# Moving the 20-token tile from the last block of each layer to the first

## The chip, the cores and the metric

The kernel runs on one core of a Trainium2 chip. Its time is the device time of one execution in microseconds (us). Five engines work side by side, each through its own list of instructions in order: TensorE (PE: matmuls and transposes; PEld is its loading of stationary operands), VectorE (DVE), ScalarE (ACT), GpSimd (POOL) and SyncE (SP). POOL issues the indirect DMAs, SP and ACT plain ones. Engines meet only through semaphores.

## The reference

Two layers of a graph transformer over 2708 tokens of 512 numbers, with 8 heads of 64, everything in float32. One layer is, in essence:

```python
mask = adj + eye(n)
q, k, v = h @ Wq.T + bq, h @ Wk.T + bk, h @ Wv.T + bv      # 8 heads
scores = q . k / 8, set to -1e9 where mask == 0
ctx = softmax(scores) @ v
h1 = layer_norm(h + ctx @ Wo.T + bo)
ff = relu(h1 @ W1.T + b1) @ W2.T + b2                      # 512 -> 2048 -> 512
h2 = layer_norm(h1 + ff)
```

The adjacency is sparse: a token has a handful of neighbours, so scores are needed for a few keys of each token only. The same adjacency serves both layers, and the output of the first is the input of the second.

## The kernel before, in words

**Tokens by rank.** The program turns each row of the adjacency into a list of neighbours, and sorts the tokens by the length of their list, longest first. The 2708 tokens make NT = 22 tiles of 128, of which the last, tile 21, holds only 20 tokens; these have the shortest lists of all. `CAPS` holds the number of list slots of each tile: 22 for tile 0, then 14, 13, 12, down to 5 for tile 20 and 3 for tile 21. `ident_i` and `idx` say which token has which rank, and which rows its neighbours are. `FIRST` is the number of tiles, from the end, whose part of these tables is made ready first (`ranked`, `listed`), so that attention can begin with them.

**Attention of a tile** goes by chunks of two slots (`SLOTS`): a POOL indirect DMA fetches for each slot one row of keys and values for each of the tile's tokens (`loads`, L1004); VectorE multiplies by q and sums over each head (L1041, L1047); one step later ACT takes the exponent and scales half of the values (L1060, L1067), and VectorE scales the other half and adds up (L1073, L1080); two and three steps later the sums are closed (L1088 to L1103) and ACT divides (L1111), which gives cx. `attend` runs this as a sequence of steps. It is advanced by credit (`advance`, `PACE`) between the pieces of other work and holds at most two finished tiles ahead; `through(k)` runs it on until block k is done. Three chunks are fetched ahead (`EARLY`), into five or more buffers.

**Blocks.** The 22 tiles are worked in 11 blocks of two, in the order of the list `blocks`, which is the subject of the change; `order` is the same list tile by tile, and attention runs through it. For a block, `attended` transposes cx (L1166), projects by Wo and normalizes to h (L1293, then `norm`: L1150 to L1160); `turned` transposes h to hT; `feed_forward` makes 16 groups pf of 128 hidden units (L1351, over the block's 256 columns at once), which ACT evicts through relu as ft (L1359), and accumulates each tile's 512 outputs in `a` (L1324), three groups late. While block k is in its feed-forward, at group 10 or 11 the next block's cx is taken, projected and normalized, so that its hT is there when block k ends. In layer 0 the keys and values of the next layer are projected for block k in the groups 5 to 8 of block k + 1 (`keys_values`, L1407, L1410), and scattered to DRAM. In layer 1 the queries of later tiles are projected inside the blocks (`queries`, L1264).

**The small tile.** A tile of at most 32 tokens fills only a quarter of TensorE's columns. For it, four matmuls of a contraction go side by side into four column groups of the array, each with its own 32 rows of the output (`project` at L571, and `quarters` at L1339); VectorE then adds the four parts, three adds more than for a full tile (`plus_rest`: L586, or L588 where a scale goes with it).

**Who sets the order.** The instruction lists of TensorE, ACT and SP follow the program text (`by_hand`). VectorE's and POOL's lists are written in the order that a scheduler chooses; VectorE's and POOL's parts at the start and between the layers lie in a `manual_schedule`, but VectorE's list still shows chunks of one tile ahead of sums of another. Once built, each list is run in order.

**The two ends.** Before the first block of layer 0, TensorE projects keys, values and queries of all tokens (L576 in `first` and `first_queries`), while VectorE and ACT make the lists. Queries of the first four tiles are made from their own rows (`own_query`, L976) and not fetched from DRAM. Between the layers, the two queries of the first tiles are projected, then the last block's keys and values, then ten more queries, two of them early, while attention of layer 1 starts; its first gathers wait for the last keys in DRAM. The output rows go out by an indirect DMA (L1379). Behind it stands a slower version of the whole program (`by_rows`), which runs only where a list is too long for its slots; here it is skipped.

Of the kernel before, what the change touches and what calls it, by code (L numbers as in the profile page):

```python
# [45 lines left out]
QT = 6  # L46
OWN = 13
EARLY = 3
FIRST = 5
PACE = (0.62, 0.72)  # L50


# [420 lines left out]
def by_edges(ctx: ExitStack, tc: tile.TileContext, x, xT, adj, layers, out, good):  # L473
# [11 lines left out]
    NT = (N + P - 1) // P  # L485
# [118 lines left out]
    def lists_of(pa):  # L604
# [151 lines left out]
        def ranked(hot, before, half):  # L756
# [49 lines left out]

            first, last = NT - FIRST, NT - 1
            rest = nc.gpsimd.dma_start(out=new[:LW, last, :], in_=rec_d[last * P :, :])
# [12 lines left out]
        def listed(start):  # L821

            ts = slice(NT - FIRST, NT) if start else slice(0, NT - FIRST)
            if not start:
# [604 lines left out]
    now = Layer(0, layers[0])  # L1429


    blocks = [(20, 19), (18, 17), (7, 9), (6, 10), (5, 11), (0, 16)]
    blocks += [(1, 15), (2, 14), (3, 13), (4, 12), (NT - 1, 8)]
    NB = len(blocks)
    order = [g for block in blocks for g in block]

# [102 lines left out]
    for n in range(NL):  # L1539
# [30 lines left out]
        for k, block in enumerate(blocks):  # L1570
# [4 lines left out]
            for f, zs in enumerate(now.feed_forward(block, hs, hT)):  # L1575
# [22 lines left out]
                if not last:  # L1598
# [9 lines left out]
                    if f == 1 and k in (1, 3):  # L1608
                        i, name, scale = (1, "bk", 1.0) if k == 1 else (0, "bq", DK**-0.5)
# [41 lines left out]
def gnn_transformer(tc: tile.TileContext, x, xT, adj, layers, out):  # L1651

    nc = tc.nc
    with tc.tile_pool(name="result", bufs=1) as result:
        good = result.tile([1, 1], F32, name="good")
        by_edges(tc, x, xT, adj, layers, out, good)  # L1660
        redo = result.tile([1, 1], I32, name="redo")
        nc.vector.tensor_scalar(redo, good, P - 0.5, None, ALU.is_lt)
        again = nc.values_load(redo[0:1, 0:1], min_val=0, max_val=1)  # L1663
        with tc.If(again > 0):
            by_rows(tc, x, xT, adj, layers, out)
# [41 lines left out]
```

## Time and profile before

| what | us |
|---|---|
| three runs: median (lowest to highest) | 1942.04 (1936.44 to 1943.61) |
| profiled execution, its own time | 1946.15 |
| span of the profile, first to last instruction | 1944.3 |
| TensorE busy / VectorE / ACT / POOL | 1858.4 / 1321.0 / 934.7 / 809.3 |
| first pf of layer 0, first pf of layer 1 | 286.8, 1232.9 |
| last matmul ends | 1925.8 |

A line of the timeline has the start, the length in us, the engine, the source line, the operation with output and inputs, the number of instructions merged into it and, in brackets, how long the engine had been idle before and what released it. A float32 matmul shows as two instructions. A line of the list of waits has the instruction that waited, what it waited for, the total, the number of times and the longest. Times are counted from the span's start.

### The profile page before, as it was taken

What the parts mean: (1) busy time and instruction counts of PE and PEld (TensorE: products, weight loads), DVE (VectorE), ACT (ScalarE), POOL (GpSimd) and SP (SyncE); (2) the same over time, 40 slices, a digit from 0 to 9 for tenths busy, and PEclk for the clock granted to TensorE, in tenths of its full rate; (3) what the DMA queues carried; (4) which work ended last, traced back from release to release, by engine and by line L of the source; (5) the groups of instructions that cost most, each with busy time, mean ns of one, the idle gap of its engine ahead of it and who ended that gap; (6) DMA issues with size and microseconds to landing.
All of it is one profiled execution on the core that took longest, in us unless ns stands there. A gap on an engine that the chain in (4) does not pass through costs nothing. (4 is left out here: it accounts for less than half of the span.)

```text
span 1944.3 us, 20898 instructions
## 1 busy us (share of the span) xinstructions
PE 1858.4 (96%) x6162; PEld 1096.7 (56%) x6162; DVE 1321.0 (68%) x2172; ACT 934.7 (48%) x3219; POOL 809.3 (42%) x710
## 2 busy tenths in 40 slices
PE   9998968999999999999999997999999999999996
PEld 4443435556656556665665553566666666666663
DVE  5885467768759687695841237696987998877421
ACT  4660236445546655574451113555475767654510
POOL 3113526535536555364410124344555775546101
PEclk9999979999999999999999998999999999999998
DMA  9998848555646656554401478656665766643000
GB/s 322 355 314 299 275 136 302 172 179 184 205 138 201 217 188 197 177 183 154 146 17 65 136 246 325 202 197 204 203 222 168 251 222 220 209 155 125 17 6 14
DMA packets 131486, 366.92 MB, mean 189 GB/s; under 512 B 16668, under 2 KB 37004, under 8 KB 128654
## 3 DMA queue, kind: packets, MB, share of 16 engines
q0 software_dynamic: 69120, 246.35, 38.0%
q1 hardware_dynamic: 53332, 99.66, 14.8%
q10 hardware_dynamic: 8910, 19.48, 2.6%
q8 instruction: 50, 0.82, 0.2%
q14 instruction: 74, 0.61, 0.1%
HBM read 314.62 MB, written 50.83 MB: 188 GB/s over the span
## 5 line engine op out<-in xcount | busy, mean ns | idle before, releaser
L1004 POOL DMA_INDIRECT kv<-kv_d,idx x420 | 547.0, 1302 | 452.2 <-DVE acc L1080 273.5
L1351 PE MATMUL pf<-hT,w 128*128 128x256 f32 (+1 forms) x2816 | 637.2, 373 | 7.2 <-ACT ft L1359 5.2
L1324 PE MATMUL a<-w,ft 128*128 128x512 f32 x1344 | 632.2, 596 | 5.3 <-ACT ft L1359 4.4
L1351 PEld LDWEIGHTS pf<-hT,w 128*128 128x128 f32 x2816 | 521.2, 191 | 186.6 <-issue 106.5
L1359 ACT ACTIVATE ft<-pf,b 128x256 f32<-128x256 f32 (+1 forms) x352 | 160.3, 460 | 458.5 <-PE pf L1351 458.3
L1041 DVE TENSOR_TENSOR kv<-kv,q 128x1024 f32<-128x1024 f32 (+3 forms) x222 | 254.2, 1157 | 169.2 <-DMA kv<-kv_d,idx 131.1
L1324 PEld LDWEIGHTS a<-w,ft 128*128 128x128 f32 x1344 | 253.2, 191 | 198.6 <-issue 171.6
L1067 ACT ACTIVATE kv<-kv,p 128x64 f32<-128x64 f32 x1232 | 311.0, 335 | 5.0
L1047 DVE TENSOR_REDUCE sc<-kv 128x16 f32<-128x1024 f32 (+3 forms) x222 | 253.8, 1153 | 1.5
L1080 DVE TENSOR_TENSOR acc<-acc,kv 128x1024 f32<-128x1024 f32 (+2 forms) x178 | 204.0, 1146 | 18.9 <-ACT kv L1067 17.0
L1156 POOL TENSOR_TENSOR rd<-va,mhalf 128x1 f32<-128x1 f32 (+1 forms) x88 | 90.4, 1028 | 274.6 <-DVE va L1154 273.7
L576 PE MATMUL o<-wo,cT 128*128 128x512 f32 x336 | 151.1, 602 | 0.5 <-ACT cT L1171 0.5
L1073 DVE TENSOR_TENSOR kv<-kv,p 128x512 f32<-128x512 f32 (+1 forms) x178 | 121.4, 682 | 34.6 <-ACT p L1060 34.6
L1060 ACT ACTIVATE p<-sc,minus 128x8 f32<-128x8 f32 x420 | 102.8, 294 | 69.2 <-DVE sc L1047 62.1
L1111 ACT ACTIVATE cx<-acc,su 128x64 f32<-128x64 f32 (+1 forms) x352 | 88.5, 334 | 74.7 <-DVE su L1103 57.6
L576 PEld LDWEIGHTS o<-wo,cT 128*128 128x128 f32 x336 | 64.5, 193 | 83.2 <-issue 72.9
L681 ACT ACTIVATE code<-aj 128x2708 bf16<-128x2708 int32 (+1 forms) x22 | 73.3, 3332 | 49.2 <-POOL aj L677 49.0
L684 DVE MAX8 tops<-code 128x8 f32<-128x247 f32 (+2 forms) x242 | 83.1, 401 | 19.3 <-ACT code L681 19.3
L1160 DVE SCALAR_TENSOR_TENSOR h<-h,rd,ln_b 128x512 f32<-128x512 f32 (+1 forms) x88 | 65.6, 747 | 40.6 <-POOL rd L1156 40.6
L1067 ACT ACTIVATE acc<-kv,p 128x64 f32<-128x64 f32 (+1 forms) x352 | 88.8, 334 | 1.4
L1410 ACT COPY kvs<-v 128x512 f32<-128x512 f32 (+1 forms) x22 | 12.9, 586 | 158.9 <-PE v L576 138.5
L1375 DVE TENSOR_TENSOR h<-a,h 128x512 f32<-128x512 f32 (+1 forms) x44 | 29.9, 679 | 85.2 <-PE a L1339 48.8
(154 smaller groups left out, 1560.2 us busy)
## 6 DMA issues: line engine op xcount, KB each, us to landing
aj<-in_adj SPq DMA_DIRECT2D x21, 1354.0 KB, 8.4
kv_d<-kvs ACTq DMA_DIRECT2D x21, 512.0 KB, 7.4
w<-in_W SPq DMA_DIRECT2D x20, 512.0 KB, 6.5
xg<-in_xT SPq DMA_DIRECT2D x19, 512.0 KB, 8.6
kv<-kv_d,idx POOLq DMA_INDIRECT x420, 5.8
w<-in_W ACTq DMA_DIRECT2D x12, 512.0 KB, 7.2
q_d<-qs SPq DMA_DIRECT2D x22, 256.0 KB, 3.4
zT_d<-zT SPq DMA_DIRECT2D x22, 256.0 KB, 4.3
```

The lines of the kernel that those rows point to most:

```text
L576: nc.tensor.matmul(o[:r], xs(c), wm[:, c, :], start=(c == 0), stop=(c == NC - 1))
L1004: nc.gpsimd.indirect_dma_start(out=to, out_offset=None, in_=table[:, :], in_offset=bass.IndirectOffsetOnAxis(ap=s, axis=0), bounds_check=N ...
L1041: nc.vector.tensor_tensor(kv[:r, :c, :DM], kv[:r, :c, :DM], self.q[:r].unsqueeze(1).to_broadcast([r, c, DM]), ALU.mult,)
L1047: nc.vector.tensor_reduce(self.sc[:r, s0 : s0 + c, :], kv[:r, :c, :DM].rearrange("p s (h d) -> p s h d", d=DK), AX.X, ALU.add,)
L1060: nc.scalar.activation(p[:r, s, :], self.sc[:r, s, :], AF.Exp, bias=minus[:r, g, s : s + 1])
L1067: nc.scalar.activation(to[:, i, hd], kv[:r, i, DM + h * DK : DM + (h + 1) * DK], AF.Copy, scale=p[:r, s0 + i, h : h + 1],)
L1073: nc.vector.tensor_tensor(to[:, 0, :].rearrange("p (h d) -> p h d", d=DK), kv[:r, 0, DM:].rearrange("p (h d) -> p h d", d=DK), p[:r, s0, : ...
L1080: nc.vector.tensor_tensor(self.acc[:r, :c, :], self.acc[:r, :c, :], kv[:r, :c, DM:], ALU.add)
L1156: nc.gpsimd.tensor_tensor(rd[:r], va[:r], mhalf[:r], ALU.pow)
L1324: nc.tensor.matmul(a[:r], fts[f][:, c0 : c0 + r], self.w2[f // 2][:, f % 2, :], start=(f == 0), stop=(f == NFC - 1),)
L1351: nc.tensor.matmul(pf[:, :w], self.w1[f // 2][:, c, f % 2 * P : f % 2 * P + P], hT[:, c, :w], start=(c == 0), stop=(c == NC - 1),)
L1359: nc.scalar.activation(ft[:, :w], pf[:, :w], AF.Relu, bias=self.b1[:, f : f + 1])
```

## The change

The list of blocks is written in another order. Tile 21 (20 tokens) with tile 20 becomes the first block of each layer; tiles 19 and 18 the second; then (8, 9), (7, 10), (6, 11), (0, 17), (1, 16), (2, 15), (3, 14), (4, 13), (5, 12). Before, tile 21 stood with tile 8 in the last block. In chunks the blocks were 6, 8, 10, 11, 11, 15, 11, 11, 10, 11, 7, and are now 5, 7, 10, 10, 11, 15, 11, 11, 10, 10, 11. `FIRST` goes from 5 to 4, since the first four tiles of the order are now the last four by rank. How the small tile is computed stays as it was.

```diff
-FIRST = 5
+FIRST = 4
...
-    blocks = [(20, 19), (18, 17), (7, 9), (6, 10), (5, 11), (0, 16)]
-    blocks += [(1, 15), (2, 14), (3, 13), (4, 12), (NT - 1, 8)]
+    blocks = [(NT - 1, NT - 2), (NT - 3, NT - 4)] + [
+        (i, NT - 5 - i) for i in (*range(8, 5, -1), *range(6))
+    ]
     NB = len(blocks)
     order = [g for block in blocks for g in block]
```

## The prediction

> **What bounds the kernel now.** I read the page's busy shares, then the list of what TensorE waited for, then TensorE's timeline through the two places where those waits lie, then VectorE's timeline there. The chain that ended last reaches back only to 1932 us (the output's scatter), so the bound is argued from TensorE. Page and waits of TensorE:
>
> ```profile
> PE 1858.4 (96%) x6162; PEld 1096.7 (56%) x6162; DVE 1321.0 (68%) x2172; ACT 934.7 (48%) x3219; POOL 809.3 (42%) x710
> ...
> PE tp L1166 <- ACT cx L1111: 25.5, 4, 14.2
> PE tp L1166 <- DVE h L1160: 10.1, 4, 3.7
> ...
> PE pf L1351 <- ACT ft L1359: 5.2, 3, 2.9
> ```
>
> TensorE works 1858 of 1944 us; some 19 us of the rest is the tail after its last matmul (1925.8 us). Elsewhere it waits mainly for attention (cx) and for the norm behind it (h), at the start of each layer. TensorE's timeline there, layer 0, then layer 1 from 1200 us:
>
> ```profile
> 263.15 1.91 PE L1166 MATMUL tp<-ident,cx 128*128 128x128 f32 x4 [14.21 <-ACT cx L1111]
> ...
> 286.81 9.03 PE L1351 MATMUL pf<-hT,w 128*128 128x256 f32 x32 [0.46 <-ACT hT L1171]
> ...
> 332.60 1.04 PE L1166 MATMUL tp<-ident,cx 128*128 128x128 f32 x8
> ...
> 357.86 0.66 PE L1166 MATMUL tp<-ident,h 128*128 128x128 f32 x4 [3.14 <-DVE h L1160]
> ...
> 365.20 7.07 PE L1351 MATMUL pf<-hT,w 128*128 128x256 f32 x32
> ...
> 1211.87 1.91 PE L1166 MATMUL tp<-ident,cx 128*128 128x128 f32 x4 [7.43 <-ACT cx L1111]
> ...
> 1232.91 7.17 PE L1351 MATMUL pf<-hT,w 128*128 128x256 f32 x32 [1.05 <-ACT hT L1171]
> ...
> 1303.59 6.64 PE L1351 MATMUL pf<-hT,w 128*128 128x256 f32 x30
> ```
>
> The rows at 286.81, 365.20, 1232.91 and 1303.59 are the starts of the first and second feed-forward block of each layer. Between 248.3 and 410 us TensorE is idle for 30 us in all, and for 14 us between 1174 and 1233. From then on it runs without a gap over 4 us. So: whatever starts the *second* block of a layer sooner, measured against the TensorE work still left, shortens the kernel. VectorE in the stretch that makes cx late:
>
> ```profile
> 253.19 1.23 DVE L1041 TENSOR_TENSOR kv<-kv,q 128x1024 f32<-128x1024 f32 x1 [4.63 <-DMA kv<-kv_d,idx]
> 260.22 0.69 DVE L1041 TENSOR_TENSOR kv<-kv,q 128x512 f32<-128x512 f32 x1 [1.21 <-DMA kv<-kv_d,idx]
> 1193.19 1.22 DVE L1041 TENSOR_TENSOR kv<-kv,q 128x1024 f32<-128x1024 f32 x1 [5.15 <-DMA q<-q_d]
> ```
>
> By buffer names these three belong to tile 18, of the second block: the scheduler put them ahead of tile 19's sums, so the first block waits for a transfer that it doesn't need.
>
> **What the skill says here.** "TensorEngine Tiling (Array Packing)", section PSUM Bottleneck: packing small matmuls speeds up TensorE and leaves the emptying of PSUM as it was. The trace agrees, and more: 64 packed matmuls of the 20-token tile (L1339) take 8.4 us, 131 ns each, against 632.2/1344 = 470 ns for a full tile (L1324); but an add of 20x512 on VectorE takes 0.68 us, as one of 128x512 does, and each packed result needs three more of them (L586, L588). So the small tile is cheap on TensorE and dear on VectorE; the forecast goes by that. "TensorE: Matmul & The Clock Gate", section on HAM oscillation, says that idle gaps above about 3.4 us drop the clock: after the 14.21 us gap four transposes took 1.91 us, not 0.60, and the granted clock was 0.65 in 250 to 260 us. I price a long gap at its length plus 1 to 2 us.
>
> **The change, part by part.**
>
> *TensorE's work* is the same in total but for 2.7 us (tile 21's own query in layer 0: 1.05 us for 3.44, and smaller transposes). It moves: with 148 columns a feed-forward block costs 37.0/2 = 18.5 us for pf and 15.0 + 4.2 us for a, 37.7 in all, against 30.0 + 30.1 = 60.1. So the first block loses 22.4 us and the last gains them; with the output projection (1.05 for 3.6 us) and transposes, **25.1 us** of work move from ahead of the second block to behind it, 27.5 in layer 1 with tile 21's query.
>
> *Attention ahead of the blocks.* A chunk is two slots. Before, the first two blocks need 6 and 14 chunks; now 5 and 12. FIRST 4 instead of 5 follows the tiles that start first; one copy smaller, nothing I price.
>
> *Layer 0, first block.* The instruction order of the changed kernel has no chunk of tile 19 ahead of tile 20's sums. Walking VectorE's list with the durations above: tile 21's first product at 221 (q needs three more adds, 2.1 us), tile 20's last chunk at 240, its sums at 246, cx on ACT by 249: where TensorE now arrives (248.3 less 2.7) and waits 2 to 3 us instead of 14.2. The projections end at 257, then VectorE has two products of tile 19 in front (4.9 us), tile 21's h with three adds (6.5) and tile 20's (4.3): 270, and the first block starts at about **272**, 15 us sooner than 286.8.
>
> *Layer 0, second block.* Here the cover is thin. TensorE would reach the transposes of cx after 12 steps of 2.1 to 2.4 us, near 300. VectorE must first do, from 270: three adds for a query, tile 19's last chunk, tile 18's four, their sums, and three chunks of tile 8 that the list puts ahead: 33.6 us by summing its list, plus about 5 us of gather waits (6 us were lost so in 300 to 320), so cx of tile 18 comes at about 308 to 310 against 325.1 (cx of tile 17). ACT holds its ft evictions in order behind that, so TensorE stands still at about the sixth to eighth step: about 15 us lost. From cx to the next block took 40 us before (325.1 to 365.2), paced by the norm's chain; I take 36, as the remaining steps are shorter: second block at **346**. Sum: 346 - 365.2 + 25.1 = **+6** us (bounds 0 to +12, as 340 or 352).
>
> *Keys and values of the first block* (L1407) then need six more adds on VectorE (4.3 us) before their PSUM is free, while TensorE gets there 4.9 us sooner (k, v of tile 21 take 2.1 us, not 7.0). Before, it waited 2.05 us there. I add **+2** (0 to +10; the list holds two chunks fewer ahead of them).
>
> *Between the layers* the last block is now full. Its norm is hidden by two queries, one of which shrinks from 3.44 to 1.05 us, so 1 to 2 us show, while tile 21's seven adds are gone from there: **+0.6**. All keys are still written by the same amount of TensorE work.
>
> *Layer 1.* The query of tile 19 is fetched on SP two q stores sooner than tile 18's was, so the 5.15 us wait should go; cx of tile 20 comes at about 1200 (layer's own time kept), TensorE's queries end at 1201, projections end at 1207, h at 1214 behind two queries: first block at **1216.6** against 1232.9. Tile 18's cx at 1249 (30 us of VectorE after the first ft, as before), TensorE there at 1246, 3 us lost; second block at **1273.5** against 1303.6. Sum: -30.1 + 27.5 = **-2.6** (bounds -8 to +4). The window for the third block's ten chunks shrinks from 82 to 70 us; VectorE needs about 64 with norms and queries (10 x 4.5 + 19): **+1.5** (0 to +6).
>
> *Tail.* VectorE's chain after the last matmul loses three adds: **-2**.
>
> Sum: 6 + 2 + 0.6 - 2.6 + 1.5 - 2 = **+5.5 us** on the profiled execution's 1946.15 us (span 1944.3 and 1.85 around it), 1951.7; that execution lies 4.1 above the median 1942.04, so **1948** as a median. Likeliest case's own range: 1940 to 1955.
>
> **Rivals.**
>
> *The early start is kept (faster).* If attention's second block keeps up with the short first one, nothing is lost: second blocks at 319 and 1265 give -21 and -11. For it: ACT and gathers have room (48%, 189 GB/s). Against: VectorE is 87% busy in 1250 to 1600, and its 33.6 us list alone ends past 300. Half of that gain, with cx of tile 18 by 300, is about -14: 1928. It decides once the second block of layer 0 starts before 338.
>
> *VectorE becomes the bound at the start (slower).* The 15 added adds of tile 21 in layer 0, 10 us, fall where VectorE is busiest instead of at the end where it idles. If gathers stall as much as in 380 to 402 us (7 us of waits), the keys' wait costs +10, the second block slips to 352 (+6 more): +19 and so 1961.
>
> *Waits at the 15-chunk block* (tile 0; 3.75 and 2.66 us near 658 and 689) stay where they are, since the block keeps its place and its 15 chunks: zero.
>
> *The change doesn't take hold:* excluded, since in TensorE's list the first pf groups now have 148 columns.
>
> **How the numbers follow.** Likeliest case 0.50, early start kept 0.17, VectorE bound 0.33. A measurement of this kernel tells about 0.5%, 9.7 us, from no change (the three runs span 7). Faster by more than that: 0.12 of the 0.17. Slower: 0.31 of the 0.33 and 0.08 of the 0.50, so 0.39. Within: 0.49. Range for 8 in 10: 1929 to 1963, from the faster rival's centre to just past the slower one's.
>
> **What would show it.** First pf near 272 and 1217, with the 14.21 and 7.43 us waits gone; new waits of pf or a for ft (L1359) in the first block of layer 0, some 15 us; second pf rows near 346 and 1273; v (L576) waiting for kvs more than 2 us; a tail of 17 us. Wrong if the list's gathers land late, if the next 10-chunk windows of layer 1 show waits, or if VectorE is simply quicker than its list.

## The result, and the profile after

The changed kernel takes 1952.62 us (median of 16 runs, 1947.54 to 1957.56), the kernel before 1942.29 us (16 runs beside it). The ratio is 1.0053, 95% interval [1.0041, 1.0065]: slower by 10.3 us, just past the 0.5% named as the limit of what can be told. The profiled execution has an own time of 1954.57 us and a span of 1952.8, against 1946.15 and 1944.3: a difference in span of 8.5, which the bookkeeping below explains.

From the page of the changed kernel and from the list of what TensorE waited for (engine, operation and line; what it waited for; us in total, times, longest):

```profile
PE 1863.1 (95%) x6162; PEld 1097.8 (56%) x6162; DVE 1321.8 (68%) x2175; ACT 933.9 (48%) x3219; POOL 805.2 (41%) x710
...
PE tp L1166 <- DVE h L1160: 23.8, 9, 6.1
PE a L1339 <- ACT ft L1359: 22.8, 8, 5.4
...
PE pf L1351 <- ACT hT L1171: 4.4, 4, 2.8
...
PE tp L1166 <- ACT cx L1111: 3.8, 1, 3.8
...
PE v L576 <- DVE kvs L586: 1.5, 1, 1.5
```

The waits for cx are down from 25.5 us to 3.8. In their place stand 22.8 us of waits for ft at L1339, the packed second matmuls of the 20-token tile, and waits for h more than twice as long as before. TensorE's timeline (start, duration, operation, wait ahead of it) shows where: layer 0's first block, the start of its second, then layer 1's.

```profile
268.53 6.75 PE L1351 MATMUL pf<-hT,w 128*128 128x148 f32 x32 [0.46 <-ACT hT L1171]
...
282.53 1.89 PE L1339 MATMUL a<-w,ft 128*20 128x512 f32 x2 [5.42 <-ACT ft L1359]
...
303.93 2.17 PE L1339 MATMUL a<-w,ft 128*20 128x512 f32 x4 [5.23 <-ACT ft L1359]
...
337.03 1.12 PE L1166 MATMUL tp<-ident,h 128*128 128x128 f32 x4 [6.12 <-DVE h L1160]
...
347.16 7.07 PE L1351 MATMUL pf<-hT,w 128*128 128x256 f32 x32
...
1227.90 4.32 PE L1351 MATMUL pf<-hT,w 128*128 128x148 f32 x32 [0.55 <-ACT hT L1171]
...
1272.62 1.03 PE L1339 MATMUL a<-w,ft 128*20 128x512 f32 x2 [4.12 <-ACT ft L1359]
...
1294.34 7.07 PE L1351 MATMUL pf<-hT,w 128*128 128x256 f32 x32
```

Between layer 0's two pf rows TensorE is idle for 22.1 of 78.6 us, and its granted clock there (the share of full speed that the profile shows) is 0.79, against 0.93 in the first block before. The packed matmuls of a (L1339) also take longer: the same 64 add up to 20.6 us instead of 8.4, since the waits break them up (a piece of two takes 1.03 us at 1235.07, an unbroken eight 1.05 at 1291.54) and, in layer 0, the clock is lower. An ft waits because ScalarE works in program order, and attention stands ahead of it. ScalarE's timeline just ahead of the 5.42 us wait:

```profile
279.66 0.49 ACT L1060 ACTIVATE p<-sc,minus 128x8 f32<-128x8 f32 x2 [4.77 <-DVE sc L1047]
280.19 2.02 ACT L1067 ACTIVATE acc<-kv,p 128x64 f32<-128x64 f32 x8
282.11 0.36 ACT L1359 ACTIVATE ft<-pf,b 128x148 f32<-128x148 f32 x1
```

ScalarE waits 4.77 us for scores from VectorE, weighs a chunk, and only then evicts ft at 282.11; 0.4 us later TensorE goes on. So the wait named "ft" is a wait for attention. VectorE works without a gap from 267 to 288.7 us. Later in the block it is not full: of the 78.6 us it is busy for 59.5, and it waits 3.7, 3.9 and 6.4 us for gathered keys and values. The longest of these waits:

```profile
323.19 1.23 DVE L1041 TENSOR_TENSOR kv<-kv,q 128x1024 f32<-128x1024 f32 x1 [6.43 <-DMA kv<-kv_d,idx]
```

No run separates VectorE's own work from the gathers that feed it; "attention" below stands for both.

Where the 8.5 us come from. The third column is plain difference; the fourth is the TensorE work that the change has moved behind that point; the sum is what the kernel has really lost or gained by then. 25.1 and 27.5 are the prediction's; k and v of the first block add 4.9 (7.0 less 2.1 us) once passed, and o with its transposes for a full last block gives 2.7 back.

| Point, us | Before | After | Difference | Work moved | Net |
|---|---|---|---|---|---|
| layer 0, second pf | 365.20 | 347.16 | -18.0 | 25.1 | +7.1 |
| layer 0, third pf | 449.55 | 423.87 | -25.7 | 30.0 | +4.3 |
| layer 0, sixth pf | 696.24 | 676.91 | -19.3 | 30.0 | +10.7 |
| layer 0, last pf | 1088.62 | 1074.05 | -14.6 | 27.3 | +12.7 |
| layer 1, first pf | 1232.91 | 1227.90 | -5.0 | 5.0 | 0.0 |
| layer 1, second pf | 1303.59 | 1294.34 | -9.3 | 27.5 | +18.2 |
| last matmul of a, end | 1925.65 | 1939.40 | +13.8 | 0 | +13.8 |
| span | 1944.3 | 1952.8 | +8.5 | 0 | +8.5 |

The prediction's 22.4 us for a block's feed-forward was 1.8 too much: layer 1's last block takes 55.3 us from pf to end with 256 columns and 34.7 with 148, a difference of 20.6. (It added up durations of rows that overlap: in the third block a pf row of 1.89 us and an a row of 1.88 start 1.7 us apart.) With 1.8 taken off, the second pf of layer 1 stands at +16.4, and layer 0's rows would be lower by as much.

A single row is not exact. Two of the runs below have, for a while, the same instruction lists as one of the two kernels, so their profiles are second profiles of it. "The small tile in the second-last block" is the kernel before up to 845 us: its second, third and sixth pf come at 358.66, 446.22 and 693.04. "The change in layer 0 alone" is the changed kernel up to 1140 us: 346.58, 423.60, 673.39, and the last pf at 1071.68. With all four pairs of profiles, the net lies between 6.5 and 13.6 us at the second pf, and between 7.2 and 13.9 at the sixth. A difference of a few us at one row can be chance.

Layer 0 loses its 12.7 us mainly in three places: the first block (7.1, of which 2.8 come back in the second), the third (4.9) and the sixth (4.6, of which 2.2 come back in the seventh). The boundary gives it back: between the last pf of layer 0 and the first of layer 1 TensorE is idle for 14.4 us before and 7.4 after, its granted clock from the end of layer 0's last block is 0.92 before and 0.98 after, and 1.8 us of it are the prediction's overcount. Most of that gain belongs to layer 1's own short block: with layer 0 alone changed, 3.6 us come back there. Layer 1's first block loses it again. The rest of layer 1 loses nothing more, and the tail gives 5.3 us.

### The profile page after: what moved, and what is told of

It reads as the page before. It is cut to its first block, busy times and chain, and to the rows that moved or that the text cites. A ratio compares the mean times of both kernels' runs of the same rounds, so it can differ in the third digit from the quotient of the medians.

```text
span 1952.8 us, 20888 instructions
## 1 busy us (share of the span) xinstructions
PE 1863.1 (95%) x6162; PEld 1097.8 (56%) x6162; DVE 1321.8 (68%) x2175; ACT 933.9 (48%) x3219; POOL 805.2 (41%) x710
## 4 chain that ended last, share of the span: by engine, by line
PE 52%; issue 3%; DVE 2%; ACT 2%; DMA 2%; POOL 1%; POOLq 0%; SPq 0%; DVEq 0%
PE pf L1351 20%; PE a L1324 20%; PE o L576 5%; PE q L576 2%; PE k L576 2%; PE v L576 2%; PE tp L1166 1%; POOL kv L1004 1%; ACT kv L1067 1%; DMA kv<-kv_d,idx 1%; DVE kv L1041 0%; DMA q<-q_d 0%; DMA zT<-zT_d 0%; DVE sc L1047 0%; ACT acc L1067 0%
## 5 line engine op out<-in xcount | busy, mean ns | idle before, releaser
L1060 ACT ACTIVATE p<-sc,minus 128x8 f32<-128x8 f32 (+1 forms) x420 | 102.9, 295 | 58.9 <-DVE sc L1047 53.0
L1417 POOL DMA_INDIRECT kv_d<-kvs,ident_i x22 | 25.2, 1147 | 156.1 <-ACT kvs L1410 100.4
```

Source lines behind the costliest of these rows:

```text
L1060: nc.scalar.activation(p[:r, s, :], self.sc[:r, s, :], AF.Exp, bias=minus[:r, g, s : s + 1])
```

## The experiments

Theory going in: the saving is lost where attention sets the pace at a layer's start, and its work comes back where TensorE does. Rivals: the packed tile's extra adds on VectorE; the new pairs and the order of VectorE's list, with the small tile innocent; TensorE as the bound throughout.

### The change in layer 0 alone

```diff
-    blocks = [(20, 19), (18, 17), (7, 9), (6, 10), (5, 11), (0, 16)]
-    blocks += [(1, 15), (2, 14), (3, 13), (4, 12), (NT - 1, 8)]
+    blocks = [(NT - 1, 20), (19, 18), (8, 9), (7, 10), (6, 11), (0, 17)]
+    blocks += [(1, 16), (2, 15), (3, 14), (4, 13), (5, 12)]
+    later = [(20, 19), (18, 17), (7, 9), (6, 10), (5, 11), (0, 16)]
+    later += [(1, 15), (2, 14), (3, 13), (4, 12), (NT - 1, 8)]
...
+                        blocks, order = later, [g for block in later for g in block]
                         pool += nxt.preloaded(order[:8], temp)
```

> Layer 0 in the changed kernel's order, layer 1 in the order of before. Theory (the small tile's saving is lost where attention sets the pace, and its work comes back where TensorE does): by the rows of TensorE layer 0 is 12.8 us behind at its end once the moved work is counted, and layer 1 with its tail gains back 4.4. So this kernel should be the slowest of the three: +12.8 us, ratio 1.0066 (1.004 to 1.009), second feed-forward block of layer 0 at 347 as in the changed kernel, tail 18.7 as before. Rival (both layers lose alike): half of the change, +4 to +5 us, 1.0025.

Measured: 1.0063 [1.0047, 1.0078], median 1954.56. Second pf of layer 0 at 346.58, last at 1071.7, last matmul at 1932.95, 19.4 us ahead of the span's end. So layer 0's half costs about 12 us by the ratio (10.2 by the medians), and layer 1's half with the tail costs nothing or gains a little. The intervals of this kernel and of the whole change overlap, so a gain of layer 1's half is not shown; what is shown is that layer 0's half by itself costs as much as the whole change.

### The small tile's place alone

```diff
-    blocks = [(20, 19), (18, 17), (7, 9), (6, 10), (5, 11), (0, 16)]
-    blocks += [(1, 15), (2, 14), (3, 13), (4, 12), (NT - 1, 8)]
+    blocks = [(NT - 1, 19), (18, 17), (7, 9), (6, 10), (5, 11), (0, 16)]
+    blocks += [(1, 15), (2, 14), (3, 13), (4, 12), (20, 8)]
```

> The small tile's place alone: the list of before with tiles 21 and 20 exchanged, so the blocks are (21,19), (18,17), ..., (20,8) and every other pair stays. Theory: the second block still waits for the attention of tile 17, of which only one chunk (some 4.5 us) is gone ahead of it, so it starts near 355 in layer 0 and the 25 us come back at the end: +16 in layer 0, +18 to +20 in layer 1 less 5 in the tail: 1.013 (1.009 to 1.018). Rival A (the cost is that of the small tile's extra adds on VectorE): as the changed kernel, 1.005. Rival B (the cost comes from the new pairs and their order, not from the small tile): no change, 0.998 to 1.001.

Measured: 1.0102 [1.0085, 1.0119]; second pf of layer 0 at 356.38 (expected: near 355). The place costs by itself more than the whole change. The pairs are not the cause, nor is `FIRST`, which stays 5 here; the change's shift of the other tiles, one chunk less in the second block, most likely hides part of the cost. Rival B falls.

### No adds for the packed parts

```diff
     def rest(o, r):
-        return [o[q * Q4 : q * Q4 + r] for q in range(1, 4)] if r <= Q4 else []
+        return []
```

> The changed kernel without the adds that sum the small tile's four packed parts (only the first part is kept, so the rows of tile 21 lack three quarters of every product). TensorE's work is unchanged. Theory: six of the adds lie ahead of the second block in each layer, 4 us; the gap to the same edit on the kernel before stays at 5 us or more, ratio 1.002 to 1.004. Rival A (the adds are the cost): the gap goes, within 2 us of the same edit on the kernel before, ratio 0.998 to 1.000.

> The kernel before without the same adds (the same part of tile 21's sums is left out). Both theories: only the three adds of the last norm (2 us) lie on the path; ratio 0.998 to 1.000. It is the base for the changed kernel without them.

Measured: changed kernel 1.0060 [1.0040, 1.0079], kernel before 0.9969 [0.9953, 0.9986]. The gap between the two is 0.91% and was 0.53%: without the adds the change costs no less. The kernel before gained 6 us where 2 were expected: its tail falls from 18.7 to 13.6 us, while the changed kernel has no packed tile in its tail. The adds are not the cost, and rival A falls. The changed kernel did not even gain the 4 us expected of six fewer adds: its second pf comes at 348.4 (347.16 with the adds), its third at 432.3 (423.87). VectorE's list came out differently there; which step of it is at fault was not followed up.

### Less attention in the second block

```diff
+    def slots(g):
+        return 3 if g in (19, 18) else CAPS[g]
+
     def chunks_of(g):
-        S = CAPS[g]
+        S = slots(g)
```

The sums use the same S. For the kernel before, the two tiles are (18, 17).

> The changed kernel with the lists of the second block's tiles (19 and 18) cut to 3 slots each: 4 chunks instead of 7 in each layer (those tiles' rows lack the other slots). Theory (attention of the second block sets when that block may start): three chunks at some 4.5 us of VectorE each are gone, the waits for ft in the first block (22.8 us) mostly go, the second block starts some 12 us sooner in layer 0 and 8 in layer 1: ratio 0.996 (0.993 to 0.999). Rival (the short first block waits for something else: the norm's chain, weights, the order on ScalarE): the waits stay and the ratio is above 1.002.

> The kernel before with the same cut in its second block (tiles 18 and 17 to 3 slots each: 4 chunks instead of 8). Theory: there the second block does not wait for attention, so little is gained: 0 to 6 us, ratio 0.997 to 1.000, and the 14.2 us wait for cx ahead of the first block stays. Rival: a gain as large as in the changed kernel (over 15 us), which would say that less attention is worth the same whatever the first block is.

Measured: changed kernel 0.9999 [0.9985, 1.0013], 10.5 us less than the change; kernel before 0.9872 [0.9851, 0.9892], 25 us less. The first was expected to close the gap. It widened, to 1.27% (the two cuts are not equal, four chunks a layer against three), and the rival written for the kernel before came true. So the theory was too narrow in two ways.

First, attention sets the pace in the kernel before as well, and well beyond the second block: with four chunks fewer its sixth pf comes at 674.3 instead of 696.24; with three chunks fewer that of the changed kernel comes at 660.2 instead of 676.91. That is 5.5 and 5.6 us a chunk (4.7 and 4.4 against the second profiles), with no TensorE work taken away. Some of the 21.9 us in the kernel before is its 14.2 us wait for cx, of which 5.4 are left.

Second, a wait in the short block is not tied to the second block's own lists. With them cut, the longest wait grows, in TensorE's timeline of the cut changed kernel (its lines lie three further down):

```profile
287.92 1.90 PE L1342 MATMUL a<-w,ft 128*20 128x512 f32 x2 [12.02 <-ACT ft L1362]
```

The main loop advances attention by 1.1 chunks at each step of the first block, so with the second block's chunks done it pulls in the third block's, and the ft written behind them waits for those. In layer 1 the same cut gained nothing between first and second pf (69.0 us against 66.4).

### A slower pace in the first block

```diff
-                advance(PACE[n] if k else 1.1 if f < 11 else 0.4)
+                advance(PACE[n] if k else 0.65 if f < 11 else 0.4)
```

> The changed kernel with attention advanced by 0.65 chunks instead of 1.1 at each of the first eleven steps of a layer's first block. Nothing is left out. ScalarE works in program order, so an ft waits for the attention work written ahead of it; with 0.65 the third block's chunks are no longer pulled into the short first block. Theory A (this pace, not the amount of attention, is what holds the short block): the waits of a for ft (22.8 us) fall below 12, the second block of layer 0 starts near 341 instead of 347, and 4 to 10 us are gained on the changed kernel: ratio 1.001 (0.999 to 1.003). Theory B (a short block hides too little attention, and chunks not done in it are waited for later): the waits move to the second and third blocks, ratio 1.004 to 1.007.

Measured: 1.0104 [1.0086, 1.0123], worse than either theory said, on the side of B. The second pf comes 1.9 and 3.0 us sooner (345.2 and 1291.4), less than A wanted. Layer 0's last pf is 2 us ahead of the changed kernel's and level with its second profile, so nothing is lost there; layer 1's third pf comes at 1373.1 instead of 1364.92, behind waits for cx and h that the changed kernel has not:

```profile
1264.71 1.91 PE L1166 MATMUL tp<-ident,cx 128*128 128x128 f32 x4 [4.52 <-ACT cx L1111]
...
1360.09 0.68 PE L1166 MATMUL tp<-ident,h 128*128 128x128 f32 x4 [3.44 <-DVE h L1160]
1363.29 1.11 PE L1166 MATMUL tp<-ident,h 128*128 128x128 f32 x4 [2.53 <-DVE h L1160]
```

Attention that isn't done in the short block is waited for in the next. The pace of 1.1 doesn't make the loss.

### VectorE in program order through layer 0's first block

```diff
-    with tc.manual_schedule(engines={mybir.EngineType.Pool}):
-        made = first(layers[0], beside_keys)
-        with tc.manual_schedule(engines={mybir.EngineType.DVE}):
-            first_queries(*made, beside_queries)
+    in_order = ExitStack()
+    in_order.enter_context(tc.manual_schedule(engines={mybir.EngineType.Pool}))
+    made = first(layers[0], beside_keys)
+    in_order.enter_context(tc.manual_schedule(engines={mybir.EngineType.DVE}))
+    first_queries(*made, beside_queries)
...
-        in_order = ExitStack()
-        if n == 0:
-            in_order.enter_context(tc.manual_schedule(engines={mybir.EngineType.Pool}))
```

> The kernel before with VectorE and GpSimd kept in program order, as one stretch, from the start to the end of layer 0's first block. Nothing is left out. The chunks of tile 18 then stand behind the sums of tile 19. Theory: the wait of 14.2 us for cx ahead of the first block shrinks to 5 or less and the first block starts 8 to 12 us sooner; how much of it reaches the end depends on the second block's attention, which has slack there: 4 to 10 us, ratio 0.996 (0.994 to 0.999). Rival (the wait is only moved into the first block): ratio 0.999 to 1.002.

> The changed kernel with VectorE and GpSimd in program order from the start to the end of layer 0's first block, the edit that took 0.41% off the kernel before. Nothing is left out. If the change is slower because its VectorE list came out worse, the two kernels should meet here (ratio within 0.2% of 0.996). If it is slower because a short block hides less attention, the edit finds no 14 us wait to remove: 0 to 4 us, ratio 1.003 to 1.006, and the gap grows to 0.8% or more.

Measured: kernel before 0.9959 [0.9947, 0.9971], the fastest here that computes all of it (1933.71 us); changed kernel 1.0104 [1.0087, 1.0121]. In the kernel before the wait for cx shrinks as said, and the first pf comes 8.9 us sooner:

```profile
254.75 1.91 PE L1166 MATMUL tp<-ident,cx 128*128 128x128 f32 x4 [5.37 <-ACT cx L1111]
...
277.86 2.50 PE L1351 MATMUL pf<-hT,w 128*128 128x256 f32 x5 [0.46 <-ACT hT L1171]
```

The second pf is at 354.8 and the sixth at 685.8, both 10.4 sooner: the gain stays. That VectorE itself stood still behind that chunk's gather, for 4.63 us at 253.19 in the kernel before, would explain a part of it. In the changed kernel the second pf also comes 7 us sooner (340.2), but the third comes at 428.1 instead of 423.87, behind waits for VectorE to empty the first block's sums out of PSUM:

```profile
350.85 1.13 PE L1324 MATMUL a<-w,ft 128*128 128x512 f32 x2 [3.61 <-DVE h L586]
...
358.67 2.08 PE L1324 MATMUL a<-w,ft 128*128 128x512 f32 x2 [6.69 <-DVE h L1375]
```

In program order these adds stand behind attention. The gap between the two kernels is now 1.45%: a bad order of VectorE's list is part of what the kernel before pays, and program order in both does not close the gap. Since program order brings the changed kernel waits of its own, this does not clear the order of the changed kernel's own list.

The same for layer 1 too, on the kernel before:

```diff
-            with tc.manual_schedule(engines={mybir.EngineType.DVE}):
-                for _ in range(2):
-                    now.query(*pool.pop(0))
+            in_order.enter_context(tc.manual_schedule(engines={mybir.EngineType.DVE}))
+            for _ in range(2):
+                now.query(*pool.pop(0))
```

> The kernel before with VectorE in program order through the first block of both layers (GpSimd in layer 0 alone). Nothing is left out. In layer 1 a chunk of tile 18 then no longer stands ahead of tile 19's sums, waiting for its query. If that is the 7.4 us wait for cx there, it shrinks to 3 or less and 3 to 6 us are gained on top of layer 0's 8: ratio 0.9935 (0.991 to 0.995). If the wait only moves into the first block: 0.996.

Measured: 0.9989 [0.9976, 1.0002]. The wait for cx in layer 1 goes from 7.4 to 4.2 us, but first to second pf then takes 78.6 us instead of 70.7, with waits for VectorE such as this one:

```profile
1283.41 1.11 PE L1166 MATMUL tp<-ident,h 128*128 128x128 f32 x4 [4.22 <-DVE h L1160]
```

A miss: the wait moved. The scheduler's freedom on VectorE helps layer 1's first block and hurts layer 0's.

### The small tile in the second-last block

```diff
-    blocks += [(1, 15), (2, 14), (3, 13), (4, 12), (NT - 1, 8)]
+    blocks += [(1, 15), (2, 14), (3, 13), (NT - 1, 8), (4, 12)]
```

> The kernel before with its last two blocks exchanged in both layers: (21,8) and then (4,12). Theory: the start of each layer is as before; only the tail changes, in which two full tiles were done 5.2 us sooner after the last matmul in the changed kernel (13.5 us against 18.7). Ratio 0.9973 (0.996 to 0.999). Rival (the packed block's norm and its keys then stand on the path elsewhere): 0.999 to 1.002.

Measured: 1.0077 [1.0058, 1.0095], against an expected gain. The tail did shrink as said, from 18.7 to 12.9 us after the last matmul (1950.0 to 1962.9; the profiled execution is this kernel's slowest, 7.5 us above its median). But both short blocks stand still, far from any layer's start:

```profile
1027.72 1.90 PE L1339 MATMUL a<-w,ft 128*20 128x512 f32 x2 [7.97 <-ACT ft L1359]
...
1854.67 2.16 PE L1339 MATMUL a<-w,ft 128*20 128x512 f32 x4 [5.86 <-ACT ft L1359]
```

Over the last two blocks of both layers and the boundary TensorE is idle for 27.8 us instead of 14.4. The block behind the short one still needs attention for two full tiles, and the short one comes to its ft steps too early for it. So it is not only the start of a layer that makes a short block dear, but attention still owed to a block behind it. Only in the last block is none owed.

### TensorE's work taken out of the first block

The last run takes from the kernel before about as much TensorE work as the change does, at the same place, by leaving out most second matmuls of the first block. The text changes nothing else; VectorE's list, which the scheduler writes, differs from 343 us on.

```diff
-                    if only not in (None, g) or r <= Q4:
+                    less = block == blocks[0] and 0 < f < NFC - 1
+                    if only not in (None, g) or r <= Q4 or less:
                         c0 += r
                         continue
                     nc.tensor.matmul(
```

> The kernel before, with 14 of the 16 second matmuls left out for both tiles of the first block of each layer (their feed-forward sums lack those parts): 28 matmuls of 0.94 us (632.2/672), 26.3 us of TensorE work less per layer at the place where the change takes 25.1, with attention, its order, the pairs and all other VectorE work as before, and nothing paid back later. Theory (up to the sixth block of layer 0, and in the first two blocks of layer 1, attention on VectorE sets the pace, and TensorE work there is about half covered): the second block of layer 0 starts some 18 us sooner, not 26; of 52.6 us of work 20 to 32 are gained: ratio 0.987 (0.9835 to 0.990). Rival A (TensorE is the bound there too, and what the change lost came from its packed tile, its order or its pairs): 45 to 53 us, 0.973 to 0.977. Rival B (that work was wholly covered): 0.997 to 1.000.

Measured: 0.9877 [0.9851, 0.9903], 23.9 us of the 52.6 taken out (19 to 29), as the theory said and far from both rivals. In the profiled execution layer 0's last pf comes at 1075.8 instead of 1088.62: 12.8 of 26.3 us are gained. The change kept 14.6 of 27.3 by that row. TensorE's timeline of the lightened first block and the start of the second:

```profile
309.76 3.78 PE L1352 MATMUL pf<-hT,w 128*128 128x256 f32 x8 [4.67 <-ACT ft L1360]
...
349.11 1.12 PE L1166 MATMUL tp<-ident,h 128*128 128x128 f32 x4 [7.73 <-DVE h L1160]
353.62 1.12 PE L1166 MATMUL tp<-ident,h 128*128 128x128 f32 x4 [3.40 <-DVE h L1160]
...
357.94 4.41 PE L1352 MATMUL pf<-hT,w 128*128 128x256 f32 x18
```

The same waits for ft and h appear with no packed tile, no new pair and no new order. The second pf comes only 7.3 us sooner (18 expected; 0.7 against the second profile of the kernel before); most of layer 0's gain appears by the third pf, 12.0 us sooner at 437.5 (8.7). The lines of this kernel lie one further down.

### What the runs say together

Sixth pf of layer 0 in the profiled executions, against the TensorE work and the attention ahead of it. Behind the stroke stands a second profile of the same lists, where there is one:

| Kernel | TensorE work less, us | Chunks through block 6 | Sixth pf, us |
|---|---|---|---|
| before | 0 | 61 | 696.2 / 693.0 |
| less work | 26.3 | 61 | 682.7 |
| in order, before | 0 | 61 | 685.8 / 680.4 |
| second block cut, before | 0 | 57 | 674.3 |
| small tile swapped | 30.0 | 60 | 681.6 |
| changed | 30.0 | 58 | 676.9 / 673.4 |
| second block cut, changed | 30.0 | 55 | 660.2 |

With the list of before, a chunk less brings the point 4.7 to 5.5 us nearer (a part of this is the shorter wait for cx), and a microsecond of TensorE work less 0.4 to 0.5 us. The change takes 30 us of TensorE work and three chunks from ahead of it and gets 19.3 us (16 to 23 with the other pairs). The work comes back behind it at full price: from layer 1's second pf to its last matmul the changed kernel takes 23.0 us more.

The two savings do not seem to add up: singly, three chunks and 30 us would give 26 to 32. The swapped list gets 14.6 us (11.4), where one chunk and 30 us would give 16 to 21. So the short block may return less than the lightened one, but the shortfall of some 5 us is as large as what two profiles of the same lists differ by at this row (3.2 to 5.4), so this is not shown. Which part of it is the block's shorter steps, each of them held by the attention written ahead of its ft, and which part is chance in VectorE's list, is not settled.

## Why the prediction was right or wrong

The sum was +5.5 us on the profiled execution; +8.5 was measured, and 1952.62 for 1948 in the median, inside the likeliest case's own range of 1940 to 1955. Its likeliest outcome, no change that can be told (0.49), was missed by little: the change is slower, to which it had given 0.39. The mechanism was the predicted one. That the sum came within 3 us is in part luck: in the table's net, its terms were off by 19 us one way and by 16 the other.

- **Layer 0, first block**: right. First pf forecast at 272, measured 268.53; the 14.21 us wait is gone altogether, not cut to 2 to 3. That the scheduler's list made most of it, by a chunk of tile 18 ahead of tile 19's sums, is shown by the in-order run, which leaves 5.37 us.
- **Layer 0, second block**: right. 346 forecast, 347.16 measured, +7.1 for +6 (the second profile of the kernel before would make it +13.6), with 13.4 us of waits for ft where 15 were forecast. But 8.1 of them come at the fourth step, not the sixth to eighth. Tile 18's cx came at 301.59, not 308 to 310, but the norm behind it waited longer (6.12 us for h), so two errors cancel.
- **Keys and values of the first block**: wrong sign, +2 forecast, -2.8 measured (the net falls from +7.1 to +4.3), v waiting 1.52 us and not over 2. Six adds on VectorE were priced as if nothing hid them; the runs without adds show that the adds are not what costs.
- **The rest of layer 0**: this is the step that failed. The prediction gave it zero. Measured: +8.4 (+6.3 in the second profile of the changed kernel). The waits at the 15-chunk block, which it left where they were, are not the main reason. Before:

```profile
658.76 0.33 PE L1166 MATMUL tp<-ident,cx 128*128 128x128 f32 x1 [3.75 <-ACT cx L1111]
...
688.90 0.66 PE L1166 MATMUL tp<-ident,h 128*128 128x128 f32 x4 [2.66 <-DVE h L1160]
```

After, with the two blocks around it:

```profile
501.04 6.25 PE L1324 MATMUL a<-w,ft 128*128 128x512 f32 x10 [2.35 <-ACT ft L1359]
...
638.03 0.80 PE L1166 MATMUL tp<-ident,cx 128*128 128x128 f32 x2 [3.75 <-ACT cx L1111]
...
669.69 1.11 PE L1166 MATMUL tp<-ident,h 128*128 128x128 f32 x4 [4.04 <-DVE h L1160]
...
751.18 0.66 PE L1166 MATMUL tp<-ident,h 128*128 128x128 f32 x4 [1.37 <-DVE h L1160]
...
759.80 2.43 PE L1351 MATMUL pf<-hT,w 128*128 128x256 f32 x10 [2.81 <-ACT hT L1171]
```

  The wait for cx at 638.03 is the same 3.75 us. The wait for h behind it is 1.4 us longer, but only 1.24 us in all in the second profile. What is new in both profiles lies on either side. From third to fourth pf the kernel takes 83.3 us (83.2 in the second profile) instead of 78.3: ScalarE waits for a softmax sum of attention and only then evicts the last ft, and behind the 2.35 us gap TensorE's granted clock is 0.76 from 500 to 507 us, although the gap is shorter than the 3.4 us that the prediction quotes.

```profile
498.61 2.02 ACT L1111 ACTIVATE cx<-acc,su 128x64 f32<-128x64 f32 x8 [7.94 <-DVE su L1103]
```

  And from sixth to seventh pf it takes 82.9 us (84.3) instead of 78.3, with the waits at 751.18 and 759.80; 2.2 us (2.5) of this come back in the next block.

The prediction took the start of the second block as the last place at which attention decides ("From then on it runs without a gap over 4 us"). That a block shows no wait does not say how far attention is ahead of it: TensorE now comes to the third block 25.7 us earlier, and there attention is late.

- **Between the layers and layer 1's first pf**: right. Forecast were +0.6 and, up to the first pf, -11.3 (-16.3 in the layer's own time, with 5.0 of work moved), -10.7 together; -12.7 was measured.
- **Layer 1, second block**: mis-sized. From first to second pf 56.9 us were forecast with 3 us lost; 66.4 were measured, with 9.4 us of TensorE idle and o at 8.83 us for 7.03. The gain of 2.6 us by the second pf became a loss of 5.5 (+18.2 less layer 0's 12.7).
- **Third block's window**: +1.5 forecast, no loss measured: from layer 1's second pf to the last matmul takes 23.0 us more, no more than the fuller last block alone (20.6 and 2.7).
- **Tail**: right in sign, too small: -2 forecast, -5.3 measured (18.7 to 13.4 us). VectorE's chain behind the last matmul is 1.9 us shorter, as forecast. Most of the rest lies with the two outputs: in the kernel before both norms end together, and the second output leaves GpSimd 3.47 us after the first is through. GpSimd's timeline, before and then after:

```profile
1936.58 1.01 POOL L1379 DMA_INDIRECT out<-h,ident_i  x1 [3.47 <-issue]
```

```profile
1940.85 1.03 POOL L1379 DMA_INDIRECT out<-h,ident_i  x1 [1.08 <-DVE h L1160]
...
1944.46 1.03 POOL L1379 DMA_INDIRECT out<-h,ident_i  x1 [1.07 <-DVE h L1160]
```

  In the changed kernel the first tile's norm starts at 1936.86, before the second one's matmuls end (1939.4), and each output leaves behind its own norm. The kernel before without the adds gets the same with the packed tile still last: a tail of 13.6 us. So it is the adds, with the order in which VectorE's list then has the two norms, that made the tail long.

Of the rivals, "the early start is kept" failed as its own condition said: the second block had to start before 338. "VectorE becomes the bound at the start" had the right engine and the wrong reason: it blamed the 10 us of added adds, which the runs clear. What binds is attention as a whole, gathers included, and it did so in the kernel before.

The statement of the Trainium skill, "TensorEngine Tiling (Array Packing)", section PSUM Bottleneck, that packing leaves the emptying of PSUM as it was, agrees with the durations in this trace (0.68 us for a 20x512 add as for a 128x512 one), but no part of the loss hangs on it.

## What to carry to other kernels

A short block is cheap only where nothing else must be made ready while it runs: here in the last block, and nowhere else that was tried. Before moving work off the busiest engine in a stretch, ask what else must be finished by the end of that stretch; where another engine was barely ahead, a microsecond removed here returned about half of itself, and the same microsecond added where the busiest engine is alone was paid in full. And a block in which the busiest engine never waits may still have no slack: the third block had no wait before, and 2.8 us of them once TensorE came to it earlier.

## What was not expected

- The wait at the head of the kernel before was no cover for anything: keeping VectorE in program order over layer 0's start, with no other edit, gives 0.41% [0.29, 0.53], while the same over both layers gives 0.11% [-0.02, 0.24].
- Moving a short block from last to second-last costs 0.77% although it shortens the tail by 5.7 us.
- Without the packed tile's adds, the changed kernel is not faster (1.0060 against 1.0053), and its third pf comes 8.4 us later. Why stays open.
